# Moving three small additions per block from GpSimd's queue to ScalarE's in a fused attention and mixture-of-experts kernel

## The chip, the cores and the metric

The kernel runs on one core of a Trainium2 chip. A core has five engines, each with its own in-order queue of instructions: TensorE (PE in the profile; PEld is its weight load), VectorE (DVE), ScalarE (ACT), GpSimd (POOL) and SyncE (SP), which here only issues transfers. The time is the device time of one execution in microseconds (us). The number that counts is the median of several executions.

## What is computed

The input x has 4 images of 256 channels and 64 by 64 pixels, so 16384 tokens of 256 numbers, all float32. Three layers follow one another, each added to its input:

```python
x = x + conv_attention(group_norm(x))     # 3x3 window: 9 keys a pixel
t = to_tokens(x)
t = t + gated_window_mean(layer_norm(t))  # tanh, sigmoid, sums over 64 tokens
t = t + moe(layer_norm(t))                # 8 experts, the best 2 of each token
```

The change lies in the first layer. With q = xn Wq + bq and k = xn Wk + bk, its logits are q . k for the nine pixels around a pixel, where a neighbour outside the image is a zero row of xn, so that its key is bk alone and its logit is q . bk. The softmax goes over all nine.

## The kernel before

The tokens are worked through in 32 blocks of 512 (NB), 8 to an image. A block is 4 tiles (NT) of 128 tokens, two image rows each. Four generators make a block, and the main loop runs them side by side, shifted: in its pass g it runs `attend(g)`, `ranks(g - 2)`, `tail(g - 1)` and `produce(g + 1)`, one step of each in turn. Between the steps, `follow` feeds in steps of a fifth stream, `experts`. A list scheduler then sets the final order of each engine's instructions by its own estimate of when inputs are ready. It also inserts the waits between engines, and waits for GpSimd's transfers in flight.

`produce` normalizes the block's pixels (L437, VectorE), multiplies them with the product Wv Wo (L455, TensorE), and copies the values out of PSUM into v (L459, ScalarE). The matrix vo has one more column than values, column C, the product Wq bk, so that column C of v holds q . bk without the part from bq. Then the three sums L468, L471 and L474 add the constant qbk = bq . bk and write the result into qdotb, a tile of 128 by 4. The value tiles are offset against the query tiles by one image row, that is by half the partitions. So the sums move 64 partitions each: L468 takes the last value tile of the block before, L471 the first three of this block, L474 the other half of all four. Last, `produce` makes q (L481 on TensorE, L485 on ScalarE).

`attend` of the next pass multiplies q with the pixels (L535) and takes the maximum (L540). It then reads qdotb, whose value every logit outside the image has:

```python
qdotb = ct[g][:, pair : pair + 2]
nc.vector.tensor_add(top, top, qdotb)      # L547
nc.vector.tensor_sub(top, qdotb, top)      # L548
```

The exponentials (L552, ScalarE), the transposes of the weights (L563) and their copy pT (L565), and the product with v (L572) follow. L576 on VectorE adds the result to xT.

`tail` does the second layer: transposes (L600, copied by ScalarE at L603), a projection (L614), tanh (L625, ScalarE), and the gate z: VectorE's L626 and L628, an exponential on ScalarE (L634), and VectorE's L635 to L640, which make wx. The window sums are the matmuls L654 and L656. GpSimd raises four numbers a token tile to the power -0.5 (L339). `tail` ends with the choice of two experts for each token.

`ranks` gives each token a row in a table by expert and scatters the block's 512 tokens twice into DRAM: 8 indirect transfers a block from GpSimd's queue (L783, `rows_in`). From the third on they wait, by the manual dependence `paced`, for a recent copy pT or an expert's activation.

`experts` works on 135 slots of 256 rows. SyncE's queue fetches a slot (L882, `sx`), TensorE transposes it (L906, copied at L910), ScalarE copies the expert's first matrix to a fixed place (L899, `w1s`), the hidden layer follows (L918, then Gelu on ScalarE at L924), then the output (L936). VectorE adds a bias and scales it into `ys`, of which there are three buffers (L940, L941). Two indirect transfers from GpSimd's queue add `ys` to the output rows in DRAM (L954). The adds of a slot wait until those of the slot before have landed.

So GpSimd's queue holds, per block, 8 scatters, some 8 adds, one L339 and the three sums. ScalarE's holds the copies and activations named above.

Of the kernel before, what the change touches and what calls it, by code (L numbers as in the profile page):

```python
# [47 lines left out]
AF = mybir.ActivationFunctionType  # L48
ALU = mybir.AluOpType
# [3 lines left out]
P = 128  # L53
# [9 lines left out]
def hybrid_block_kernel(ctx: ExitStack, tc: tile.TileContext, ins: dict, out: bass.AP):  # L63
    nc = tc.nc
    x = ins["x"]
    B, C, HW = x.shape
# [3 lines left out]
    NT = TB // P  # L70
# [291 lines left out]
    qbk = const.tile([P, 1], FP, tag="qbk", name="qbk")  # L362
# [37 lines left out]
    def image_norm(b):  # L400
        mv = w2p.tile([P, NC, 2], FP, tag="imv", name=f"imv_{b}")
        for c in range(NC):
            nc.vector.bn_aggr(mv[:, c, :], stats[b][:, c].rearrange("p i s -> p (i s)"))
        mean = w2p.tile([P, NC], FP, tag="imean", name=f"imean_{b}")
        nc.vector.tensor_copy(mean, mv[:, :, 0])
        gm = ps_a.tile([P, NC], FP, tag="a", name=f"gm_{b}")
        nc.tensor.matmul(gm, gavg, mean, start=True, stop=True)

        spread = w2p.tile([P, NC], FP, tag="ispread", name=f"ispread_{b}")
        nc.vector.tensor_sub(spread, mean, gm)  # L410
        nc.vector.tensor_mul(spread, spread, spread)
        nc.vector.tensor_add(spread, spread, mv[:, :, 1])
        gv = ps_a.tile([P, NC], FP, tag="a", name=f"gv_{b}")
        nc.tensor.matmul(gv, gavg, spread, start=True, stop=True)


        vc = w2p.tile([P, NC], FP, tag="ivc", name=f"ivc_{b}")
        nc.vector.scalar_tensor_tensor(vc, gv, EPS, mv[:, :, 1], ALU.mult, ALU.add)
        rc = w2p.tile([P, NC], FP, tag="irc", name=f"irc_{b}")
        rsqrt_v(rc, vc, EPS * EPS, NC, f"c{b}")  # L420
        norm[b] = (mean, rc)
# [4 lines left out]
    def produce(g):  # L426
        if g >= NB:
            return
        b, i = divmod(g, NBI)
        if i == 0:  # L430
            image_norm(b)
        mean, rc = norm[b]
        t = xn[g] = xt.pop(g)
        lo = W if i == 0 else 0
        hi = XW - W if i == NBI - 1 else XW
        for c in range(NC):
            tc.keep_in_program_order(nc.vector.tensor_scalar(  # L437
                t[:, c, lo:hi], t[:, c, lo:hi], mean[:, c : c + 1], rc[:, c : c + 1],
                ALU.subtract, ALU.mult,
            ))  # L440
        if lo:
            nc.gpsimd.memset(t[:, :, 0:lo], 0.0)
        if hi < XW:
            nc.gpsimd.memset(t[:, :, hi:XW], 0.0)
        yield


        v = vp.tile([P, NT, C + 1], FP, tag="v", name=f"v_{g}")
        vt[g] = v
        if i == 0:  # L450
            v0[b] = w1p.tile([P, C + 1], FP, tag="v0", name=f"v0_{b}")
        for j in range(0 if i == 0 else 1, NT + 1):
            ps = ps_a.tile([P, C + 1], FP, tag="a", name=f"psv_{g}_{j}")
            for ci in range(NC):
                nc.tensor.matmul(  # L455
                    ps, t[:, ci, j * P : (j + 1) * P], vo[:, ci, :],
                    start=(ci == 0), stop=(ci == NC - 1),
                )
            nc.scalar.copy(v[:, j - 1, :] if j else v0[b], ps)  # L459
            if j == 2:  # L460
                yield
        yield

        first = v0[b] if i == 0 else vt[g - 1][:, NT - 1, :]
        qdotb = w2p.tile([P, NT], FP, tag="qdotb", name=f"qdotb_{g}")
        ct[g] = qdotb
        H = P // 2
        nc.gpsimd.tensor_scalar(  # L468
            qdotb[0:H, 0:1], first[H:P, C : C + 1], qbk[H:P], None, ALU.add
        )  # L470
        nc.gpsimd.tensor_scalar(  # L471
            qdotb[0:H, 1:NT], v[H:P, 0 : NT - 1, C], qbk[H:P], None, ALU.add
        )
        nc.gpsimd.tensor_scalar(qdotb[H:P, :], v[0:H, :, C], qbk[0:H], None, ALU.add)  # L474

        q = w2p.tile([P, NC, TB], FP, tag="q", name=f"q_{g}")
        qt[g] = q
        for co in range(NC):
            ps = ps_a.tile([P, TB], FP, tag="a", name=f"psq_{g}_{co}")
            for ci in range(NC):  # L480
                nc.tensor.matmul(  # L481
                    ps, qk[:, ci, co * P : (co + 1) * P], t[:, ci, W : W + TB],
                    start=(ci == 0), stop=(ci == NC - 1),
                )
            nc.scalar.activation(q[:, co, :], ps, AF.Identity, bias=qb[:, co : co + 1])  # L485
            if co == NC - 1:

                tc.keep_in_program_order(nc.vector.tensor_add(
                    xT[g], xT[g], outb.unsqueeze(1).to_broadcast([P, NT, C])
                ))  # L490
            yield
# [505 lines left out]
    for _ in produce(0):  # L997
        pass
# [20 lines left out]
    for g in range(NB + 2):  # L1019
        load_xs(g + AHEAD + 2)  # L1020
        channel_stats(g + AHEAD)
        gens = [attend(g), ranks(g - 2), tail(g - 1), produce(g + 1)]
        if g == 1:
            load_experts()
        n = 0
        while gens:
            for gen in list(gens):
                if next(gen, gens) is gens:
                    gens.remove(gen)
                    continue  # L1030
                n += 1
                follow(g + min(n / STEPS.get(g, 26), 0.999))
# [51 lines left out]
```

## Time and profile before

| | us |
|---|---|
| median of 3 executions | 1412.79 |
| lowest and highest | 1408.81, 1413.75 |
| the profiled execution's own time | 1404.04 |
| its span, first to last instruction | 1402.3 |
| mean granted TensorE clock | 0.971 |
| TensorE busy | 1271.8 (91%) |
| TensorE weight loads | 1053.7 (75%) |
| VectorE busy | 989.7 (71%) |
| ScalarE busy | 772.4 (55%), 1509 instructions |
| GpSimd busy | 772.5 (55%), 711 instructions |
| the three sums, 96 instructions on GpSimd | 36.1 |

The profile describes one execution. A group of instructions is named by its line, engine, operation, and output and input tiles. "Idle before" is the time for which the engine stood still just ahead of the group, followed by what it waited for. A wait for several things is put down to the one that came last by the profile, so that the name can be wrong when that thing had long been done. The share of busy time is a mean over stages with different limits: the start (the first image is loaded and its statistics are made), the long middle in which blocks and experts run together, and the end, where only experts are left.

### The profile page before, as it was taken

To read this page: it belongs to the slowest core of one execution; us is meant where nothing else is said; L and a number is where in the kernel's file an instruction comes from. 1 tells how busy PE (TensorE), PEld (TensorE's weight loads), DVE (VectorE), ACT (ScalarE), POOL (GpSimd) and SP (SyncE) were. 2 spreads that over 40 slices of the span, in tenths; PEclk is the share of its full clock that TensorE was granted. 3 is DMA by queue.
4 is the path that set the end of the run, shared out by engine and by line. 5 is a ranking of instruction groups with operands and counts; after the bars stand their busy time and mean duration, and the time that the engine had idled before them with its cause. 6 is when DMAs were issued, how large, how long until landed. Compare 5 with 4: busy or idle time off the path is not lost. (4 is left out here: it accounts for less than half of the span.)

```text
span 1402.3 us, 23444 instructions
## 1 busy us (share of the span) xinstructions
PE 1271.8 (91%) x6224; PEld 1053.7 (75%) x6224; DVE 989.7 (71%) x4649; ACT 772.4 (55%) x1509; POOL 772.5 (55%) x711
## 2 busy tenths in 40 slices
PE   5898999999999999999999999999999999777761
PEld 4677777888888877888888878888888888555550
DVE  4599979787877787787878787787867788522221
ACT  1334357766666665676667655666666665323220
POOL 2133535556566666656566556666665666655444
PEclk8999999999999999999999999999999999889896
DMA  9724455555665655565555555555566555565543
GB/s 329 256 96 136 132 168 127 135 148 138 154 149 135 155 128 139 135 166 139 145 131 134 140 138 115 119 140 138 123 136 125 112 110 114 127 146 87 82 70 37
DMA packets 147794, 190.44 MB, mean 136 GB/s; under 512 B 13776, under 2 KB 121936, under 8 KB 147536
## 3 DMA queue, kind: packets, MB, share of 16 engines
q0 software_dynamic: 51168, 71.07, 28.5%
q1 hardware_dynamic: 94000, 116.42, 26.9%
q10 hardware_dynamic: 2496, 1.45, 0.4%
q8 instruction: 52, 0.85, 0.3%
q14 instruction: 78, 0.64, 0.2%
HBM read 98.31 MB, written 90.59 MB: 135 GB/s over the span
## 5 line engine op out<-in xcount | busy, mean ns | idle before, releaser
L954 POOL DMA_INDIRECT out<-ys,sx x270 | 435.2, 1612 | 312.0 <-DVE ys L940 78.5
L936 PE MATMUL psy<-w,h 128*128 x1080 | 290.0, 391 | 74.2 <-DVE ys L940 70.7
L783 POOL DMA_INDIRECT rows_in<-tok,rows x256 | 255.6, 998 | 102.5 <-issue 67.4
L936 PEld LDWEIGHTS psy<-w,h 128*128 128x128 f32 x1080 | 202.9, 193 | 129.2 <-DVE ys L940 95.2
L918 PE MATMUL psh<-xc,w1s 128*128 128x256 f32 x1080 | 269.9, 394 | 0.3 <-DVE ys L940 0.3
L940 DVE TENSOR_TENSOR ys<-psy,b2b 128x256 f32<-128x256 f32 x270 | 113.3, 420 | 178.1 <-DMA out<-ys,sx 104.7
L918 PEld LDWEIGHTS psh<-xc,w1s 128*128 128x128 f32 x1080 | 207.6, 198 | 28.8 <-issue 1.0
L924 ACT ACTIVATE h<-psh,w1s 128x256 f32<-128x256 f32 x270 | 116.6, 477 | 161.5 <-PE psh L918 136.9
L910 ACT COPY xc<-ptx 128x512 f32<-128x512 f32 x135 | 79.5, 589 | 129.0 <-PE ptx L906 79.4
L455 PE MATMUL psv<-vo,x 128*128 128x257 f32 x528 | 128.2, 386 | 12.6 <-DVE x L437 8.9
L481 PE MATMUL psq<-x,qk 128*128 128x512 f32 x256 | 123.6, 592 | 0.0
L535 PE MATMUL pss<-x,q 128*128 128x256 f32 x512 | 122.7, 382 | 0.1
L572 PE MATMUL psc<-v,pT 128*128 128x256 f32 x512 | 121.9, 380 | 0.7 <-issue 0.4
L455 PEld LDWEIGHTS psv<-vo,x 128*128 128x128 f32 x528 | 98.8, 193 | 28.3 <-issue 8.5
L572 PEld LDWEIGHTS psc<-v,pT 128*128 128x128 f32 x512 | 96.4, 189 | 28.8 <-issue 8.4
L535 PEld LDWEIGHTS pss<-x,q 128*128 128x128 f32 x512 | 95.1, 191 | 13.8 <-ACT xc L603 1.0
L941 DVE TENSOR_SCALAR ys<-ys,sx 128x256 f32<-128x256 f32 x270 | 99.8, 370 | 4.5 <-issue 0.2
L924 ACT ACT_TABLE_LOAD x78 | 100.1, 1283 | 1.4
L552 ACT ACTIVATE pe<-logits,stop 128x259 f32<-128x259 f32 x128 | 64.3, 503 | 55.8 <-DVE stop L548 21.4
L576 DVE SCALAR_TENSOR_TENSOR xT<-psc,den,xT 128x256 f32<-128x256 f32 x128 | 55.6, 475 | 51.0 <-PE psc L572 50.2
L471 POOL TENSOR_SCALAR qdotb<-v,qbk 64x3 f32<-64x3 f32 x32 | 12.2, 382 | 140.9 <-ACT v L459 61.6
L603 ACT COPY xc<-ptx 128x512 f32<-128x512 f32 x64 | 35.8, 581 | 96.8 <-PE ptx L600 73.6
(187 smaller groups left out, 2311.0 us busy)
## 6 DMA issues: line engine op xcount, KB each, us to landing
sx<-rows_in SPq DMA_DIRECT2D x135, 272.0 KB
xs<-in_x SPq DMA_DIRECT2D x32, 512.0 KB
xT<-in_xT SPq DMA_DIRECT2D x32, 512.0 KB
out<-xT SPq DMA_DIRECT2D x32, 512.0 KB
x<-in_x SPq DMA_DIRECT2D x24, 640.0 KB
x<-in_x SPq DMA_DIRECT2D x8, 576.0 KB
out<-ys,sx POOLq DMA_INDIRECT x270
rows_in<-tok,rows POOLq DMA_INDIRECT x256
```

The costliest lines, as they stand in the source:

```text
L455: nc.tensor.matmul(ps, t[:, ci, j * P : (j + 1) * P], vo[:, ci, :], start=(ci == 0), stop=(ci == NC - 1),)
L481: nc.tensor.matmul(ps, qk[:, ci, co * P : (co + 1) * P], t[:, ci, W : W + TB], start=(ci == 0), stop=(ci == NC - 1),)
L535: nc.tensor.matmul(ps, q[:, ci, t * P : (t + 1) * P], t_[:, ci, t * P : t * P + NK], start=(ci == 0), stop=(ci == NC - 1),)
L572: nc.tensor.matmul(ps[:, u, :], pT[:, u, j, :], vals[j], start=(j == 0), stop=(j == 1))
L783: dispatch(paced(nc.gpsimd.indirect_dma_start(out=rows_in[:, :], out_offset=bass.IndirectOffsetOnAxis(ap=rows[:, c, t : t + 1], axis=0), i ...
L910: nc.scalar.copy(xc, pt)
L918: nc.tensor.matmul(ps[:, f, :], w1s[:, o : o + P], xc[:, ci, :], start=(ci == 0), stop=(ci == NC - 1),)
L924: inst = nc.scalar.activation(h[:, f, :], ps[:, f, :], AF.Gelu, bias=w1s[:, F1 + f : F1 + f + 1])
L936: nc.tensor.matmul(ps[:, t, :], h[:, f, t * P : (t + 1) * P], w2[:, e, f, :], start=(f == 0), stop=(f == NC - 1),)
L940: nc.vector.tensor_add(ys[:, t, :], ps[:, t, :], b2b[:, e, :])
L941: nc.vector.tensor_scalar_mul(ys[:, t, :], ys[:, t, :], xs[:, t, bass.ds(e + C, 1)])
L954: inst = nc.gpsimd.indirect_dma_start(out=out, out_offset=bass.IndirectOffsetOnAxis(ap=xs[:, t, C + E : C + E + 1].bitcast(U32), axis=0), ...
```

## The change

The three sums of a block are made by activations with the function Identity and a per-partition bias on ScalarE. Before, they were tensor_scalar additions on GpSimd. Operands, results and their place in the program text stay the same.

```diff
-        nc.gpsimd.tensor_scalar(
-            qdotb[0:H, 0:1], first[H:P, C : C + 1], qbk[H:P], None, ALU.add
-        )
-        nc.gpsimd.tensor_scalar(
-            qdotb[0:H, 1:NT], v[H:P, 0 : NT - 1, C], qbk[H:P], None, ALU.add
-        )
-        nc.gpsimd.tensor_scalar(qdotb[H:P, :], v[0:H, :, C], qbk[0:H], None, ALU.add)
+        nc.scalar.activation(
+            qdotb[0:H, 0:1], first[H:P, C : C + 1], AF.Identity, bias=qbk[H:P]
+        )
+        nc.scalar.activation(
+            qdotb[0:H, 1:NT], v[H:P, 0 : NT - 1, C], AF.Identity, bias=qbk[H:P]
+        )
+        nc.scalar.activation(qdotb[H:P, :], v[0:H, :, C], AF.Identity, bias=qbk[0:H])
```

## The prediction

> **What bounds the kernel now.** I read the page's shares and slices first, then the busy time in three stages, then who waited for whom in each stage, then the chain that ended last, and last the order of events around the three sums.
>
> ```profile
> PE 1271.8 (91%) x6224; PEld 1053.7 (75%) x6224; DVE 989.7 (71%) x4649; ACT 772.4 (55%) x1509; POOL 772.5 (55%) x711
> ...
> 0.00:200.00 200.00, 169.73 (x788) 134.15 (x789) 151.38 (x723) 77.12 (x191) 59.92 (x115) 0.97 0.58 191
> 200.00:1190.00 990.00, 968.97 (x4886) 812.60 (x4886) 781.90 (x3734) 643.12 (x1211) 604.89 (x523) 1.00 0.57 134
> 1190.00:1402.00 212.00, 133.09 (x552) 106.90 (x551) 56.45 (x194) 52.18 (x108) 107.72 (x75) 0.85 0.51 92
> ```
>
> The last three lines give a stretch of the span, then the busy us of TensorE, its weight loads, VectorE, ScalarE and GpSimd, the granted clock, the DMA share and GB/s. From 200 to 1190 us TensorE is busy for 968.97 of 990 us at full clock: this stage is TensorE's, and all that any other engine can give there is its idle 21 us. After 1190 it is busy for 133 of 212.
>
> ```profile
> PE psy L936 <- DVE ys L940: 13.7, 16, 1.9
> ...
> DVE ys L940 <- DMA out<-ys,sx: 104.7, 25, 5.7
> ...
> DMA 5%; DVE 1%; PE 1%; issue 1%; POOL 1%; POOLq 0%; DVEq 0%
> DMA out<-ys,sx 5%; PE psy L936 1%; DVE ys L940 1%; POOL out L954 1%; DVE ys L941 0%; POOLq L1080 0%; DVEq L940 0%; POOLq L954 0%
> ```
>
> The first line (us, times, longest) is TensorE's largest wait from 200 to 1190 us. The second is VectorE's in the whole span; asked by stage, all 25 of these waits lie after 1190 us, none before. So until then no add (L954) is late for anyone. The last two lines are the chain of waits: the end of the kernel is a chain of adds, each waiting for the one before to land (3.75 us apiece). The three sums are last run at 1123 us, so the end only moves with the moment at which it starts.
>
> ```profile
> L471 POOL TENSOR_SCALAR qdotb<-v,qbk 64x3 f32<-64x3 f32 x32 | 12.2, 382 | 140.9 <-ACT v L459 61.6 <-DMA rows_in<-tok,rows 50.7 <-ACT pT L565 18.3
> ...
> 572.43 0.97 POOL L783 DMA_INDIRECT rows_in<-tok,rows  x1 [0.31 <-issue]
> 577.22 0.53 POOL L471 TENSOR_SCALAR qdotb<-v,qbk 64x3 f32<-64x3 f32 x1 [3.82 <-DMA rows_in<-tok,rows]
> 577.84 0.40 POOL L474 TENSOR_SCALAR qdotb<-v,qbk 64x4 f32<-64x4 f32 x1
> 578.33 0.29 POOL L468 TENSOR_SCALAR qdotb<-v,qbk 64x1 f32<-64x1 f32 x1
> 578.90 1.65 POOL L954 DMA_INDIRECT out<-ys,sx  x1 [0.28 <-POOL qdotb L468]
> ...
> 571.75 0.37 ACT L459 COPY v<-psv 128x257 f32<-128x257 f32 x1
> 572.18 1.14 ACT L899 COPY w1s<-w1b 128x514 f32 x2
> 573.34 1.28 ACT L634 ACT_TABLE_LOAD   x1
> 574.63 0.21 ACT L634 ACTIVATE z<-z 128x4 f32<-128x4 f32 x1
> 576.92 0.69 ACT L485 ACTIVATE q<-psq,qb 128x512 f32<-128x512 f32 x1 [2.08 <-PE psq L481]
> ...
> 575.26 0.17 DVE L635 TENSOR_SCALAR z<-z 128x4 f32<-128x4 f32 x1
> ```
>
> This is one block of the middle (start, duration, in brackets the idle time before). GpSimd's queue stands still for 3.82 us in front of the sums, since the scheduler lets them wait for the scatters in flight; the values themselves were ready at 572.1. On ScalarE the same place, behind the last copy of v, is followed by work without a gap, up to 2.08 us of idleness before q.
>
> **The change, part by part.**
>
> *GpSimd loses* 96 instructions (36.1 us: 13.4, 12.2 and 10.5) and the idle time before them (38.1, 140.9 and 3.9 us). Behind them in its queue stand scatters and adds, which now go 2 to 5 us earlier in each block. Who waits for those? For adds, nobody before 1190 us. For scatters, the fetch of a slot, and TensorE waited for fetched rows twice in the span (5.6 us, both before 190 us). At the second of these, the fetch at 179.1 us follows the block's last scatter at 176.0. Its first two scatters stood behind the sums until 166.3, though their rows were ready at 164.5; but the third came 0.30 us after the copy pT that paces it, at 168.98, and that stays. In the changed order each scatter waits for the transfer eight before it instead; these are 8 us old or more and took under 4 to land. So this part gives 0 us, with the whole of TensorE's idleness that could hang on it as the other end: 13.7 + 5.6 = 19.3 us gained.
>
> *ScalarE gains* 96 activations of 64 partitions by 1, 3 and 4. Nearest rows: 168 ns (L380, 128x1), 191 (L718, 128x4), 206 (L634, 128x4), none with a per-partition bias. The bias costs some 90 ns (L485, 128x512 with bias, 687; L565, 128x512 copied, 597). Neighbours overlap by 0.10 us (four L681 take 2.07 us, not 4 x 0.590). So three cost 3 x 0.28 - 3 x 0.10 = 0.54 us, and with 0.1 us for the wait on the copy just ahead 0.65 us a block, 21 us in all. Ends: 3 x 0.168 = 0.5 and 3 x 0.30 + 0.2 = 1.1 us, 16 to 35 us in all. No activation table is added: L485 and L681 use Identity beside Gelu and Exp without a load of their own, and the changed program has the same 156 loads. No wait on another engine comes with them either: in the changed order they wait for ScalarE's own copies alone, and the copies of v no longer wait for GpSimd.
>
> *What is queued behind them on ScalarE:* w1s, the table load, the exponential z (L634), then q. Before q ScalarE idles by 1.2 to 2 us in most blocks, so that q and all behind it start as before. Only z can be late, and VectorE's L635 waits for it. I took, for every block, the time from z's end to L635's start. In the first six blocks it is 0.03 us, but in four of them ScalarE itself idles before z, waiting for VectorE; the cost there is at most about 0.5 us in all. In the 26 others it is 1.2 to 2.2 in eleven, 0.4 to 0.9 in seven and 0.19 to 0.34 in seven (and 0.03 in one where nothing new stands ahead). In the changed order the tight ones have two sums before z (some 0.45 us), the roomy ones three. The lateness over the slack adds up to 1.4 us; at the dear end, 0.8 us for two, it is 5.6. Behind VectorE, wx is done at least 4 us before L654 needs it from 230 us on (but for the last two blocks, which have no new sums ahead). What is left is L940, for which TensorE waits at times: I let two thirds of 1.4 + 0.5 through, 1.3 us.
>
> *The consumer:* VectorE's L547 reads qdotb in the next pass, more than 10 us later; it comes 3 to 5 us earlier than before. 0.
>
> *Order.* The scheduler also swaps neighbours elsewhere: L485's second half goes ahead of a w1s copy in some blocks, and L499 ahead of L635. TensorE's order differs in one transpose near the eighth block, SyncE's not at all. These are swaps of 0.2 to 0.6 us, of either sign: 0, with 2 us to both sides.
>
> *A rule against the row.* GpSimd's sums last 0.30 us undisturbed (their medians), 28.8 us for 96, and took 36.1: 7.3 us in which something held them up. The Trainium skill (SBUF — State Buffer, section Who interferes with whom) says that a VectorE instruction with two inputs in SBUF and a GpSimd instruction that reads SBUF block one another, the later fully. By that rule the sums also held up VectorE, by 28.8 us at most, and the change would give some of it back; in this trace L547 shows it faintly, if at all (median 160 ns, longest 275). By the rule the sum would be a gain (a rival, below), by the rows nothing.
>
> **The sum:** 0 + 1.3 + 0 = 1.3 us on the profiled execution's 1404.04. That execution lies 8.75 us under the median, so for the median I take 1412.8 + 1.3, about 1414.
>
> **The rivals.**
>
> *Faster, by GpSimd's queue.* The scatters and adds that come earlier let TensorE's waits shrink in a way that the waits, put down to the last of several, do not show. For: 183 us of idleness in front of the sums, and the adds are a chain with only about 1 us to spare at 1177 us, where the end begins. Against: no wait of VectorE on an add before 1190 us. At most 19.3 us; half of it gives 1403.
>
> *Faster, by VectorE.* If each of the 96 sums blocked VectorE in full, it has 28.8 us back; TensorE sees of it no more than its 13.7 us of waits on VectorE: 1399.
>
> *Slower, by ScalarE.* The sums stand in one place, between v and z; if VectorE's order leaves no slack where I counted it, every late z passes on through L635 to L940 and so to TensorE. With 0.65 us in each of 32 blocks it is 21 us: 1434; with a third of that 1420. It decides from 0.22 us a block on (7 us). For: nine of the middle blocks have under 0.45 us of slack. Against: TensorE's waits on ScalarE are under 1 us in the middle, and q's idle time catches the delay every block.
>
> **How the numbers follow.** Half a per cent, 7 us, is about what can be told from no change. No change 0.60 (1414, own range 1408 to 1420); faster by GpSimd's queue 0.13 and by VectorE 0.05; slower by ScalarE 0.22, since its delay is certain and only its cover is in doubt. Reaching into both sides until a tenth is left out on each, the range is 1402 to 1424; these cases give 0.18, 0.60 and 0.22.
>
> **What the changed profile would show.** ScalarE busy for 788 to 807 us with 1605 instructions; GpSimd near 736 with 615, and no 3 to 4 us gap between the second and third scatter; the three activations at 0.17 to 0.30 us; TensorE's 968.97 of 990 us within 5; L635 waiting for z in some ten more blocks, by under 0.5 us each; the chain of adds as long as before (25 waits, 105 us). I am wrong if VectorE's waits on ScalarE or TensorE's on L940 grow by over 7 us, or if TensorE's waits on L940 go and the end starts that much earlier.

## The result, and the profile after

The changed kernel takes 0.9912 of the time of the kernel before (95% interval 0.9885 to 0.9939; medians 1396.38 and 1410.89 us, six runs each, side by side). A second comparison on another occasion gave 0.9897 (0.9859 to 0.9934). So it is faster by about 1%, where 1.3 us slower had been forecast: 12.4 us by the ratio, 14.5 us by the medians, and 15.5 us by the medians of the second occasion (1400.29 and 1384.80 us).

The page of the changed kernel (busy us of each engine), then the same three stages as before (stretch of the span, then TensorE, weight loads, VectorE, ScalarE, GpSimd, granted clock, DMA share, GB/s):

```profile
PE 1267.5 (91%) x6224; PEld 1052.1 (76%) x6224; DVE 988.8 (71%) x4649; ACT 801.9 (58%) x1605; POOL 737.3 (53%) x615
...
0.00:200.00 200.00, 169.45 (x788) 134.71 (x789) 150.98 (x723) 83.90 (x214) 53.30 (x93) 0.96 0.57 191
200.00:1190.00 990.00, 975.41 (x4922) 818.85 (x4921) 787.57 (x3768) 667.76 (x1288) 581.56 (x452) 1.00 0.59 135
1190.00:1402.00 212.00, 122.68 (x517) 98.55 (x516) 50.26 (x160) 50.23 (x104) 102.44 (x70) 0.86 0.50 88
```

Span 1393.4 us against 1402.3. In the middle stage TensorE is busy for 975.41 us where it was 968.97; the last stage, a fixed 1190 to 1402 us, has less left to do. Next, TensorE's largest wait from 200 to 1190 us, VectorE's wait for adds in the whole span, and VectorE's wait for the exponential z (us in all, times, longest):

```profile
PE psy L936 <- DVE ys L940: 7.7, 17, 1.4
...
DVE ys L940 <- DMA out<-ys,sx: 97.0, 24, 5.6
...
DVE z L635 <- ACT z L634: 4.2, 12, 0.5
```

TensorE's wait on L940 fell from 13.7 to 7.7 us. VectorE waits for adds a little less than before (25 waits and 104.7 us there), but the end as a whole, from the last L338 (VectorE's instruction ahead of the power, once a block) to the last instruction, takes 238 us where it took 239. ScalarE's cost is there: L635 waits for z 12 times, 5 times before.

One block of the changed kernel, in order of time (start, duration, idle before in brackets; instructions between them are left out, here and in the fences like it below):

```profile
409.49 1.00 POOL L783 DMA_INDIRECT rows_in<-tok,rows  x1 [1.94 <-ACT v L459]
409.84 0.43 ACT L459 COPY v<-psv 128x257 f32<-128x257 f32 x1
410.30 0.29 ACT L471 ACTIVATE qdotb<-v,qbk 64x3 f32<-64x3 f32 x1
410.60 0.30 ACT L474 ACTIVATE qdotb<-v,qbk 64x4 f32<-64x4 f32 x1
410.80 0.98 POOL L783 DMA_INDIRECT rows_in<-tok,rows  x1 [0.30 <-issue]
413.43 1.61 POOL L954 DMA_INDIRECT out<-ys,sx  x1 [1.65 <-DVE tmv_a L499]
413.46 0.20 ACT L634 ACTIVATE z<-z 128x4 f32<-128x4 f32 x1
413.69 0.29 ACT L468 ACTIVATE qdotb<-v,qbk 64x1 f32<-64x1 f32 x1
413.70 0.17 DVE L635 TENSOR_SCALAR z<-z 128x4 f32<-128x4 f32 x1 [0.46 <-ACT z L634]
```

The three activations last 0.29 to 0.30 us and follow each other at 0.30. Two of them delay z by 0.46 us here, as the prediction had it. GpSimd has no sums left to stand still for.

**Where the time came from.** Compared instruction by instruction, the changed kernel is 1.5 us late until 190 us, level at 200, and then ahead by about a microsecond more in each block up to 575 us (8 to 9 us), which it keeps to the end. (The two profiled executions differ by 8.9 us, less than the medians, since the one of the kernel before took 1404.04 us, less than each of its six timed ones; what follows accounts for these 8.9 us.) The steps lie in TensorE's stalls before L936, where it waits for L940. But VectorE was late there long before L940. The next two fences show one place in the kernel before and the same place in the changed one:

```profile
399.58 1.24 PE L535 MATMUL pss<-x,q 128*128 128x256 f32 x5
400.65 1.89 PE L918 MATMUL psh<-xc,w1s 128*128 128x256 f32 x8
400.67 1.28 ACT L924 ACT_TABLE_LOAD   x1
401.42 1.60 POOL L954 DMA_INDIRECT out<-ys,sx  x1 [0.30 <-DVE nt_f L353]
402.38 1.03 PE L936 MATMUL psy<-w,h 128*128 x4
403.09 1.08 POOL L339 TENSOR_TENSOR trstd_a<-ve_a,nhalf 128x4 f32<-128x4 f32 x1
403.31 0.48 DVE L540 CUSTOM_DVE_ANT_0 logits<-pss,mask,pads 128x256 f32<-128x256 f32 x1 [1.60 <-PE psh L918]
403.40 0.47 ACT L924 ACTIVATE h<-psh,w1s 128x256 f32<-128x256 f32 x1 [1.45 <-PE psy L936]
```

```profile
397.42 1.89 PE L918 MATMUL psh<-xc,w1s 128*128 128x256 f32 x8
397.49 1.28 ACT L924 ACT_TABLE_LOAD   x1
398.29 0.47 DVE L540 CUSTOM_DVE_ANT_0 logits<-pss,mask,pads 128x256 f32<-128x256 f32 x1
398.59 1.56 POOL L954 DMA_INDIRECT out<-ys,sx  x1 [0.31 <-DVE trstd_f L355]
399.35 0.48 ACT L924 ACTIVATE h<-psh,w1s 128x256 f32<-128x256 f32 x1 [0.58 <-PE psh L918]
```

In the kernel before, the only thing that L540 waits for is its scores (L535), done at 400.82. VectorE is free at 401.71, yet L540 starts at 403.31. ScalarE's L924 has its table at 401.95 and its matmuls at 402.55, yet starts at 403.40. Both start 0.3 to 0.4 us behind the end of the add L954 (403.02), just behind which the power L339 starts. In the changed kernel GpSimd is some 7 us earlier relative to the rest, the power has long run at 392.56, and L540 starts without a gap. The names in the brackets (L918, L936) are those of work that merely ended nearby.

To look for more of these I counted, from 195 to 1190 us, the starts of VectorE and ScalarE after more than 0.3 us of idleness that no other engine's end explains: no TensorE signal due within 0.2 us before, and no end of another compute engine within 0.12 us. Their sum is called the marker below. It holds idle time of other causes too, so it marks holds and does not price them, and its sums hang on these limits by up to 3 us. In the kernel before there are 25 of them with 28.8 us, and 18 (an expectation below says 19) start 0.15 to 0.42 us behind the start of L339, which there follows the end of an add within 0.07 us. In the changed kernel there are 11 with 13.5 us.

A caution belongs to all that follows. The profiles of before, after and e1 to e4 lack a part of the semaphore updates (the signals between engines): the one of the kernel before has 1185 of the 1337 that TensorE's matmuls send, and 3205 of VectorE's 3949. The profiles of e5 to e12, taken on another chip than e1 to e4, have practically all. Places like L540's above, where an instruction that waits for nothing else starts 0.3 to 0.4 us behind an add's end, appear in all six incomplete profiles (21 in the kernel before, 7 in the changed one, 4 to 11 in the others) and in none of the eight complete ones, two of which have no adds. The kernel before was timed on that chip (the gain is the same there) but not profiled. So markers may be compared within the six or within the eight, and whether the holds come with the chip, or with the recording that lost signals, is not known.

### The profile page after: what moved, and what is told of

It is laid out like the page before. It is cut to its first block, busy times and chain, and to the rows that moved or that the text cites. A ratio compares the mean times of both kernels' runs of the same rounds, so it can differ in the third digit from the quotient of the medians.

```text
span 1393.4 us, 23310 instructions
## 1 busy us (share of the span) xinstructions
PE 1267.5 (91%) x6224; PEld 1052.1 (76%) x6224; DVE 988.8 (71%) x4649; ACT 801.9 (58%) x1605; POOL 737.3 (53%) x615
## 3 DMA queue, kind: packets, MB, share of 16 engines
q10 hardware_dynamic: 2496, 1.45, 0.4%
## 5 line engine op out<-in xcount | busy, mean ns | idle before, releaser
L954 POOL DMA_INDIRECT out<-ys,sx x270 | 430.6, 1595 | 382.3 <-DVE ys L940 76.0
L783 POOL DMA_INDIRECT rows_in<-tok,rows x256 | 261.0, 1020 | 192.2 <-ACT v L459 66.6
L936 PE MATMUL psy<-w,h 128*128 x1080 | 292.1, 393 | 66.4 <-DVE ys L940 61.1
L936 PEld LDWEIGHTS psy<-w,h 128*128 128x128 f32 x1080 | 202.7, 193 | 121.6 <-DVE ys L940 88.0
L918 PE MATMUL psh<-xc,w1s 128*128 128x256 f32 x1080 | 263.6, 387 | 0.3 <-DVE ys L940 0.3
L940 DVE TENSOR_TENSOR ys<-psy,b2b 128x256 f32<-128x256 f32 x270 | 113.1, 419 | 170.6 <-DMA out<-ys,sx 97.0
L918 PEld LDWEIGHTS psh<-xc,w1s 128*128 128x128 f32 x1080 | 204.8, 196 | 27.9 <-issue 1.0
L924 ACT ACTIVATE h<-psh,w1s 128x256 f32<-128x256 f32 x270 | 116.9, 478 | 163.8 <-PE psh L918 129.2
L910 ACT COPY xc<-ptx 128x512 f32<-128x512 f32 x135 | 79.6, 590 | 122.3 <-PE ptx L906 55.3
L535 PE MATMUL pss<-x,q 128*128 128x256 f32 x512 | 122.7, 383 | 0.0
L535 PEld LDWEIGHTS pss<-x,q 128*128 128x128 f32 x512 | 95.6, 192 | 13.1 <-issue 0.5
L906 PE MATMUL ptx<-ident,sx 128*128 128x128 f32 x540 | 82.7, 275 | 7.9 <-DMA sx<-rows_in 7.9
L906 PEld LDWEIGHTS ptx<-ident,sx 128*128 128x128 f32 x540 | 67.0, 145 | 26.2 <-issue 11.3
```

The source lines that it names most:

```text
L535: nc.tensor.matmul(ps, q[:, ci, t * P : (t + 1) * P], t_[:, ci, t * P : t * P + NK], start=(ci == 0), stop=(ci == NC - 1),)
L783: dispatch(paced(nc.gpsimd.indirect_dma_start(out=rows_in[:, :], out_offset=bass.IndirectOffsetOnAxis(ap=rows[:, c, t : t + 1], axis=0), i ...
L906: nc.tensor.transpose(pt[:, c, t * P : (t + 1) * P], xs[:, t, c * P : (c + 1) * P], ident)
L918: nc.tensor.matmul(ps[:, f, :], w1s[:, o : o + P], xc[:, ci, :], start=(ci == 0), stop=(ci == NC - 1),)
L924: inst = nc.scalar.activation(h[:, f, :], ps[:, f, :], AF.Gelu, bias=w1s[:, F1 + f : F1 + f + 1])
L936: nc.tensor.matmul(ps[:, t, :], h[:, f, t * P : (t + 1) * P], w2[:, e, f, :], start=(f == 0), stop=(f == NC - 1),)
```

## The experiments

First set. Theory P: the power L339 is what holds the others up. Theory Q: the sums themselves do. Theory S: the scheduler's new orders on VectorE (46 places) and ScalarE made the gain.

**e1_both.** GpSimd works as before, ScalarE's sums are in use.

```diff
         nc.scalar.activation(qdotb[H:P, :], v[0:H, :, C], AF.Identity, bias=qbk[0:H])
+        spare = w2p.tile([P, NT], FP, tag="spare", name=f"spare_{g}")
+        nc.gpsimd.tensor_scalar(spare[0:H, 0:1], first[H:P, C : C + 1], qbk[H:P], None, ALU.add)
+        nc.gpsimd.tensor_scalar(spare[0:H, 1:NT], v[H:P, 0 : NT - 1, C], qbk[H:P], None, ALU.add)
+        nc.gpsimd.tensor_scalar(spare[H:P, :], v[0:H, :, C], qbk[0:H], None, ALU.add)
```

> The changed kernel, and beside ScalarE's sums GpSimd makes the three old sums as well, in the old place and with the old wait for the scatters in flight, into a spare tile that nobody reads; the orders of TensorE, VectorE and ScalarE are those of the changed kernel. Theory P (the power L339, which stands behind the sums in GpSimd's queue, holds up VectorE and ScalarE until some 0.3 us after its start, and by GpSimd's lateness falls into the softmax): GpSimd is late again, the power starts some 11 us behind L338 as before, and the time goes back to 1406 to 1414. Theory Q (it is the sums themselves that hold VectorE up): 1406 to 1414 too. Theory S (the scheduler's new order on VectorE and ScalarE, 46 places on VectorE, made the gain): stays at 1393 to 1400.

Measured 1.0001 of the kernel before (0.9977 to 1.0024): all of the gain is gone. GpSimd's idleness in front of the spare sums is 190 us (183 in front of the sums before). S falls, and with it any benefit from the orders. The power comes 8.3 us behind L338 (median from the seventh block on; 8.0 in the kernel before, not 11 as the expectation says, and 3.1 in the changed one), the marker is 25.3 us, and TensorE waits as it did before:

```profile
PE psy L945 <- DVE ys L949: 14.8, 20, 2.1
```

(The added lines shift L936 and L940 by nine.)

**e2_nowait.** The same, but on partitions that bring no wait for scatters:

```diff
-            spare[0:H, 1:NT], v[H:P, 0 : NT - 1, C], qbk[H:P], None, ALU.add
+            spare[0:H, 1:NT], v[0:H, 0 : NT - 1, C], qbk[0:H], None, ALU.add
```

and likewise the other two.

> As e1_both, but the three spare sums read and write partitions 0 to 63 only; from the scheduler they then get no wait for the scatters in flight (their values are not the sums, and nobody reads them). GpSimd has the old work without the old 3.8 us of standing still. Theory P: what counts is when the power comes; it stays early, 1394 to 1401. Theory Q: the sums are back, and so is the time, 1403 to 1414. Theory S: 1393 to 1400.

Measured 0.9860 (0.9824 to 0.9896). GpSimd does three additions a block and the gain stays whole. GpSimd's idleness in front of them is 90 us, nearly all of it for their values. Q falls: their work beside VectorE costs nothing that can be seen, their wait does. The power comes 3.0 us behind L338.

**e3_before_nopow and e4_after_nopow.** The power is taken out, in the kernel before and in the changed one:

```diff
-        nc.vector.tensor_scalar_add(ve[:, :n], var, eps)
-        nc.gpsimd.tensor_tensor(out_, ve[:, :n], nhalf[:, :n], ALU.pow)
+        nc.vector.tensor_scalar(out_, var, -0.36130995, 1.3509454, ALU.mult, ALU.add)
```

> The kernel before, in which the reciprocal root of the first token norm is not made by the power on GpSimd (L339) but by a straight line through the variance, in VectorE's one instruction L338 (within some 1% rms of the true value, so the routing hardly moves). The sums stay on GpSimd with their waits. Theory P: the stalls that end 0.3 us after the power's start (19 of VectorE and ScalarE from 195 to 1190 us, 19 us in sum) are gone: 1396 to 1404. Theories Q and S: the power is hidden, 1406 to 1414.

> The changed kernel with the same straight line in place of the power. Theory P: the stalls that the power still makes there (eight of VectorE, 0.4 to 0.8 us each, in a place where VectorE waits for TensorE anyway, and two at ScalarE or VectorE of 2.7 us) go: 1389 to 1398. Theories Q and S: no change, 1393 to 1400.

Measured 0.9968 (0.9947 to 0.9988) and 0.9892 (0.9856 to 0.9928). P expected most of the gain from the first and got a third of it. The same kind of place in e3_before_nopow, now without a power:

```profile
482.42 1.60 POOL L954 DMA_INDIRECT out<-ys,sx  x1 [0.30 <-issue]
483.61 1.03 PE L936 MATMUL psy<-w,h 128*128 x4
484.37 0.48 DVE L540 CUSTOM_DVE_ANT_0 logits<-pss,mask,pads 128x256 f32<-128x256 f32 x1 [2.14 <-PE psh L918]
484.52 0.47 ACT L924 ACTIVATE h<-psh,w1s 128x256 f32<-128x256 f32 x1 [1.11 <-PE psh L918]
```

L540 starts 0.35 us behind the add's end (484.02) again. So the power is not needed for such a place: it stood behind the add, and its start only marked the add's end. The marker there is still 20.7 us. P falls as the main cause (where the third comes from stays open), and theory L takes its place: the *adds* hold the others up when they come late in the block.

**e5_after_again, e6_one_wait.** The changed kernel again, and the changed kernel with one of e1_both's spare sums, the one that carries the wait:

```diff
+        spare = w2p.tile([P, NT], FP, tag="spare", name=f"spare_{g}")
+        nc.gpsimd.tensor_scalar(
+            spare[0:H, 1:NT], v[H:P, 0 : NT - 1, C], qbk[H:P], None, ALU.add
+        )
```

> The changed kernel as it is, beside the others on one chip. Both theories below: 0.985 to 0.994 of the kernel before, as measured first (0.9912).

> The changed kernel with one spare sum a block on GpSimd (64 partitions by 3, from partitions 64 to 127, into a tile that nobody reads), which gets the old wait for the scatters in flight; a third of the old sums' work, all of their standing still. Theory L (lateness: GpSimd's standing still puts the scatters and adds behind it some 8 to 10 us later in the block, beside the softmax, and there VectorE and ScalarE are held up until just behind the end of an add): back to the kernel before, 0.996 to 1.002 of it. Theory W (the work of the sums beside VectorE): a third of the way, 0.992 to 0.997.

Measured 0.9897 and 0.9899 (0.9861 to 0.9936). L's number was missed: one sum with the full wait costs nothing. But the power came only 6.2 us behind L338, not 8.3, and the marker is 1.3 us. Judged by the power, being 3 us later than the changed kernel is free here, and being 5 us later (e1_both) is not. One sum with the wait leaves GpSimd idle for 169 us in front of it and costs nothing, so standing still is not enough by itself. In this execution of the changed kernel the marker is 0.8 us where it had been 13.5, and its middle (table below) is 9 us shorter: the same program, held in an incomplete profile and not in a complete one.

**e7_before_noadds, e8_after_noadds.** Both kernels without the adds:

```diff
         def add(m, ys, xs):
+            return
             k, n = of[m]
```

> The kernel before without its indirect adds (L954): the experts' shares are computed and not added to the output, so the chain of adds at the end is gone as well. To be read against the next run, of the changed kernel without them. Theory A (under L, the adds are what holds the others up): the two differ by under 3 us. Theory B (under L, the scatters are it): they differ by 8 us or more, as with the adds. Either way some 1290 to 1340 us, since VectorE waits 105 us for adds at the end.

> The changed kernel without its indirect adds. Theory A: within 3 us of the run before it. Theory B: 8 us or more below it.

Measured 1292.27 and 1290.32 us, which differ by 2.0 us. That is theory A's number: without adds, GpSimd's sums with their wait and ScalarE's sums are worth the same, though everything else that the change does is still in them. TensorE's wait on L940 from 200 to 1190 us, without the adds in the kernel before and in the changed one:

```profile
PE psy L936 <- DVE ys L940: 4.6, 9, 1.0
```

```profile
PE psy L936 <- DVE ys L940: 3.8, 7, 1.0
```

The marker is 1.1 and 1.2 us. So the effect needs the adds. It is not shown that they act by holding others up: without them GpSimd's queue is so short that the power comes 0.2 and 0.3 us behind L338 in the two kernels. The sums stand still as long as ever (192 us of idleness in front of them), but the scatters are hardly late either, so theory B has not been put to the test. This pair also prices the rest of the change: in it, ScalarE's sums do not cost anything that can be told from nothing.

**e9_nine, e10_fourteen.** Lateness without any wait: the changed kernel with small sums in e2_nowait's manner, repeated.

```diff
+        for _ in range(9):   # 14 in e10_fourteen
+            nc.gpsimd.tensor_scalar(
+                spare[0:H, 1:NT], v[0:H, 0 : NT - 1, C], qbk[0:H], None, ALU.add
+            )
```

> The changed kernel with nine spare sums a block on GpSimd in the old place (64 partitions by 3, read from partitions 0 to 63, no wait for scatters, into a tile that nobody reads): some 5 us of GpSimd's time a block, no standing still. Theory L2 (what counts is how late the adds come in the block, whatever makes GpSimd late; with one spare sum and its wait the power came 6.2 us behind L338 and cost nothing, with all three 8.3 us and cost all): the power comes 7 to 8 us behind L338, 0.990 to 1.000 of the kernel before. Theory D (it is the wait for the scatters in flight, and the bunching of transfers behind it): stays at 0.986 to 0.993.

> The same with fourteen spare sums, some 7.7 us a block. Theory L2: the power comes 9 to 11 us behind L338, as in the kernel before or later: 0.996 to 1.004 of it. Theory D: 0.986 to 0.993.

Measured 0.9988 (0.9971 to 1.0006) and 1.0297 (1.0267 to 1.0327), with the power 5.5 and 12.6 us behind L338 (expected 7 to 8 and 9 to 11). Both lose the gain without any wait for scatters, so lateness alone can cost; but neither shows L2's holds. With fourteen the price is three times the gain of the change, and TensorE's waits grow (L942 and L946 are L936 and L940, L924 is L918, L735 is L729):

```profile
PE psy L942 <- DVE ys L946: 18.9, 17, 4.2
PE psh L924 <- DVE ys L946: 6.8, 1, 6.8
PE gv L414 <- DVE ispread L412: 4.8, 2, 3.4
...
DVE tok L735 <- DMA rows_in<-tok,rows: 29.1, 9, 5.8
DVE tok L735 <- issue: 7.2, 1, 7.2
```

The last two lines are VectorE's, from 200 to 1190 us. L735 writes the row numbers into tok, whose former contents the late scatters still have to read. These waits are some 36 us of this run's marker of 38.1: a wait that the profile names, and for scatters, not a hold by adds. In the kernel before L729 waits for 0.7 us in all, so this is not what the change removed.

Nine loses elsewhere. Its profiled execution is 14.0 us longer than e5_after_again's on the same chip, and 8.1 us of that lie ahead of the seventh L338 (214.8 us against 206.7): TensorE waits there 9.1 us for fetched rows, where it waits 4.3 in e5_after_again. The middle is only 3.3 us longer (marker 1.2 us), and the end has the rest. What speaks against D is thus e6_one_wait, which has the wait for the scatters and loses nothing.

**e11_behind_pow.** The kernel before, its three sums behind the power in GpSimd's queue, by a dependence in program order alone; no other engine's order changes.

```diff
-        nc.gpsimd.tensor_scalar(
+        def sums(qdotb=qdotb, first=first, v=v):     # called in attend, behind norm1[g]
+            behind_pow(nc.gpsimd.tensor_scalar(
...
+    def behind_pow(inst):
+        if pows:
+            tc.add_manual_dep(inst.ins, pows[-1].name, ...)
```

> The kernel before, with its three sums on GpSimd as they were, but put behind the power (L339) in GpSimd's queue; the orders of TensorE, VectorE, ScalarE and SyncE are those of the kernel before, and nothing is left out. They get their wait for the transfers in flight there. Theory L2: the adds ahead of the power come early in the block, as in the changed kernel: 0.986 to 0.994 of the kernel before. Theory D, and theory S' (ScalarE's sums or the orders that came with them give part of it after all): 0.996 to 1.002.

Measured 1.0144 (1.0121 to 1.0167): slower than either theory had it, so its time tells nothing between them. The reason is one that the expectation left out. The sums now come too late for L547 (here L562), which waits for them:

```profile
DVE stop L562 <- POOL qdotb L485: 28.4, 17, 3.9
```

The power comes 3.4 us behind L338 and the marker is 1.4 us. That does not bear L2 out either: in the complete profiles the marker is as small with the power 6.2 us late.

**e12_two_one.** Only the two sums that read partitions 64 to 127 go to ScalarE, as in the change; L474 stays on GpSimd.

```diff
         nc.scalar.activation(
             qdotb[0:H, 1:NT], v[H:P, 0 : NT - 1, C], AF.Identity, bias=qbk[H:P]
         )
-        nc.scalar.activation(qdotb[H:P, :], v[0:H, :, C], AF.Identity, bias=qbk[0:H])
+        nc.gpsimd.tensor_scalar(qdotb[H:P, :], v[0:H, :, C], qbk[0:H], None, ALU.add)
```

> A version of the change: the two sums that read partitions 64 to 127 (L468, L471) on ScalarE, the third (L474), which gets no wait for scatters, on GpSimd; nothing is left out. Theory L2: as the changed kernel, 0.985 to 0.992 of the kernel before, since GpSimd does not stand still. Theory W (the sums' work on GpSimd costs): a third of the gain is lost, 0.991 to 0.996.

Measured 0.9936 (0.9916 to 0.9956). The number is W's, the middle is L2's: 908.3 us against 907.8 in e5_after_again, and TensorE waits on L940 for 4.8 us. The loss against the changed kernel lies ahead of the seventh block (its seventh L338 comes at 211.5 us, against 206.7 in e5_after_again and 208.6 in the first profile). Whether that repeats isn't settled. No version tried beats the changed kernel beyond the intervals.

All runs together. The last column is the time from VectorE's seventh L338 to its 31st in the profiled execution, that is the middle alone. The first six rows are the incomplete profiles, the last eight the complete ones:

| | of the kernel before | L338 to L339, us | marker, us | middle, us |
|---|---|---|---|---|
| before | 1 | 8.0 | 28.8 | 924.8 |
| after | 0.9912 | 3.1 | 13.5 | 917.0 |
| e1_both | 1.0001 | 8.3 | 25.3 | 930.1 |
| e2_nowait | 0.9860 | 3.0 | 9.5 | 912.6 |
| e3_before_nopow | 0.9968 | none | 20.7 | 927.8 |
| e4_after_nopow | 0.9892 | none | 6.6 | 913.4 |
| e5_after_again | 0.9897 | 3.0 | 0.8 | 907.8 |
| e6_one_wait | 0.9899 | 6.2 | 1.3 | 907.9 |
| e9_nine | 0.9988 | 5.5 | 1.2 | 911.1 |
| e10_fourteen | 1.0297 | 12.6 | 38.1 | 950.4 |
| e11_behind_pow | 1.0144 | 3.4 | 1.4 | 930.4 |
| e12_two_one | 0.9936 | 3.6 | 1.2 | 908.3 |
| e7_before_noadds | 0.9237 | 0.2 | 1.1 | 907.4 |
| e8_after_noadds | 0.9225 | 0.3 | 1.2 | 906.5 |

Among the first six, the kernels with the power 8 us late (and e3_before_nopow, with the sums' wait) have a middle of 925 to 930 us, the others 913 to 917. Among the last eight the middle is 907 to 911 us with and without adds, but for e10_fourteen, which waits for scatters, and e11_behind_pow, which waits for its sums. Nothing here tells how long the middle of the kernel before is on that chip.

## Why the prediction was wrong

**The step that failed** is "GpSimd loses ... So this part gives 0 us". Its other end, 19.3 us gained, was the nearer: 12 to 15 us came. That the scatters and adds would go 2 to 5 us earlier was right (the power, which shares their queue, comes 4.9 us earlier relative to L338). The step then asked who *waits* for them, found no wait of VectorE on an add before 1190 us, and put their lateness at nothing. The finding holds, the conclusion doesn't. e1_both, where GpSimd's sums and their standing still come back beside all else of the change, loses the whole gain; e2_nowait, with sums that don't stand still, keeps it. So the lateness of GpSimd's queue behind the three standing sums cost 12 to 15 us. (One such sum, in e6_one_wait, makes the queue less late and costs nothing.)

By which way the lateness reaches TensorE is known only in part. In the two profiled executions TensorE's wait on L940 falls by 6.0 us of the 8.9. The trace of before also had a sign: L540 with 1.60 us of idleness put down to L918, which it doesn't need. That an add which nobody waits for can be in the way while it runs is argued from such places. e7 and e8 fit it, but show only that the effect needs the adds in the queue, and no complete profile has such a place. e9_nine and e10_fourteen show two other ways in which lateness can cost, by the start and by scatters that VectorE waits for. So the way stays open.

The end starts 8.3 us earlier (by the last L338) and is as long as forecast. With TensorE's smaller waits on L940 this comes close to the last sign of being wrong that the prediction names.

**The power was left out.** The step listed scatters and adds behind the sums and not L339, which gives the clearest measure of how late GpSimd is.

**ScalarE: right in kind, too cheap in size, and free.** The three activations take 0.88 us a block (28.2 us in all by the groups' 9.5, 9.4 and 9.3), not 0.65, inside the stated ends. The overlap of 0.10 us taken from larger tiles doesn't exist for these: L474 starts 0.30 us behind L471, which takes 0.29. L635 waits for z 12 times for up to 0.5 us (forecast: some ten more than the 5 before); of the 1.3 us that was to be passed on, e8 against e7 shows nothing.

**Consumer and order: right at 0.** In the changed kernel L547 waits for no sum, and e1_both, with all orders of the changed kernel, has none of its gain.

**The rule on the shared SBUF access.** The Trainium skill (SBUF — State Buffer, section Who interferes with whom) made the sums' disappearance a gain. e2_nowait, with three sums back beside VectorE and none of the gain lost, shows nothing of it here.

**The rivals.** The one that came true is "faster, by GpSimd's queue", with a chance of 0.13, in the form in which it was put: waits that the profile, putting them down to the last of several, does not show. Its way is borne out in so far as TensorE's wait on L940 shrank. Against it stood only the absence of a wait by name. Of the signs, busy times, counts and the missing gap came as predicted; TensorE's 968.97 us in the middle moved by 6.4 instead of up to 5.

## What to carry to other kernels

An instruction that stands still at the head of a queue moves everything behind it; ask where in the block the transfers behind it land, even if no semaphore ties anyone to them. An idle gap whose named releaser the instruction does not need is the sign to look for: compare its start with the ends on *all* engines, and count first whether the trace has all the signals that the instructions send. A sum of such gaps has to be opened before it is compared: in e10_fourteen it was a wait with a name. A cheap test of lateness is to give the freed queue useless work again, with and without its wait.

## What the runs showed of the hardware

In six profiles VectorE *and* ScalarE start some instructions only 0.3 to 0.4 us behind the end of an indirect add (1.6 us, L954), after idleness that nothing else they wait for explains (2.14 us in the fence of e3_before_nopow). In the kernel before, 18 of the 25 starts counted above lie there. The Trainium skill (SBUF — State Buffer, section Who interferes with whom) says that TensorE and ScalarE never wait on anyone. That is said of SBUF ports, and ScalarE's L924 with 1.45 us at 403.40 does not speak against it, since nothing shows that it waited at a port. It may have waited for a late signal: in the kernel before no update of VectorE, ScalarE or TensorE is on record from 401.14 to 403.29 us, and then three of TensorE's come within 0.15 us (403.29, 403.38, 403.44). But this trace lacks 152 of TensorE's 1337 updates and 744 of VectorE's 3949, so that a pause and a loss of records look the same in it. In the eight complete profiles no such start is found.

Many adds hold nobody: VectorE's L540 often starts while one runs. Which of them do, and why the same program has a marker of 13.5 us in one execution and 0.8 in another, stays open.

A GpSimd sum that reads partitions 64 to 127 gets a wait for the transfers in flight from the scheduler, one that reads partitions 0 to 63 does not (e12's L474, e2's sums). Between e1_both and e2_nowait this makes 100 us of GpSimd's idleness, 3.1 us a block, where the work of the three sums is 1.1 to 1.3: the wait is the larger part of the lateness that they caused.
